# First attention of a hybrid block: another way for one transpose, mask and maximum in one operation, and TensorE's order as written

## The chip, the cores and the metric

The kernel runs on one core of one Trainium2 chip. A core has five engines that run side by side and wait for each other by semaphores: TensorE (PE; its weight loads are listed apart as PEld), VectorE (DVE), ScalarE (ACT), GpSimd (POOL) and SyncE (SP), which here only issues transfers between DRAM and the on-chip memory. TensorE writes to PSUM, eight banks of 512 fp32 numbers for each of 128 partitions; the other data is in SBUF. The metric is the device time of one execution in microseconds, the median of several.

## The reference

The program is one block on `x` of shape (4, 512, 512): `x += attention_a(layernorm(x))`, then a feed-forward with ternary weights, then a second attention with block-scaled weights, then the feed-forward again. The change is inside the first of the four. Cut to what it computes (16 query heads, 4 key heads that each serve a group of 4, width 128):

```python
q, k, v = x @ Wq, x @ Wk, x @ Wv                    # per head
qs, ks = softmax(q, -1), softmax(k, -1)             # over the head's width
gl = log_sigmoid(k) / 16
def step(S, inp):                                   # over the 512 positions
    q_t, k_t, v_t, g_t = inp
    S = S * exp(g_t)[..., None] + k_t[..., None] * v_t[..., None, :]
    return S, einsum('bhk,bhkv->bhv', q_t, S)
_, o_gla = scan(step, S0, (qs, ks, v, gl))
scores = rotary(q) @ rotary(k).T * 128 ** -0.5      # causal mask, softmax
y = softmax(where(causal, scores, min)) @ v
return (0.5 * y + 0.5 * o_gla).reshape(b, n, -1) @ Wo
```

## The kernel before

`first_attention_gentle` works on the sequence in chunks of 128 rows. The scan becomes matrix products: inside a chunk with queries and keys that carry the decay up to their row (`qd`, `kd`), across chunks with a `state` for each chunk. There are 16 groups, one for each of 4 sequences and 4 key heads, and 4 chunks in a group, so 64 chunks; chunk number `c` in its group sees `c + 1` blocks of keys.

A group (class `Group`) projects keys and values (`project`, four times), makes the gates (`gates`, L386 on), the decays (`decays`: two matmuls, `down`, `held`, rotated keys `kr`, decayed keys `kd`), transposes `kr` and `kd` (`transposes`) and makes the states (`states`). A chunk (class `Chunk`) goes through seven stages:

- `A`: projection of four query heads, `mm<-wq,xnT`, copied by ScalarE to `q_t`.
- `B`: softmax of the queries times decay, `qd` (L338 to L344), and rotated queries `qr` (L329 to L332, half of it on GpSimd).
- `C`: `qr` and `qd` are transposed by TensorE, four 128x128 transposes each (L350), and copied out of PSUM by ScalarE (L351) to `qrT` and `qdT`.
- `own`: scores of the decayed queries and keys inside the chunk (L458), masked by VectorE (L460).
- `D(h)`, for each of four heads: scores (L468), the causal mask added to the last 128 columns in PSUM (L469), the negated row maximum (L472), exponential with sum (L475), reciprocal, division (L477), a transpose of 32x32 blocks by VectorE into `turned` (L478). With the last head, one transfer writes `turned` to DRAM as `passed` (L481).
- `E`: four transfers read `passed` back as `prT`, so that the blocks land transposed (L487).
- `F`: GpSimd adds `own` to the last block (L493); TensorE multiplies queries by state (`pv<-qdT,state`, L496, not for `c = 0`) and adds `c + 1` products of values and weights (`pv<-prT,v_t`, L498); ScalarE halves and copies (L500).
- `G`: output projection, `mm<-wo,oT`, added to the residual by VectorE (L186).

A loop over `n` from -7 to 65 writes one step for each chunk: in step `n` chunk `n - 2` does `G`, `n - 1` does `F`, `n` does `E` and `own`, `n + 1` does `D`, `n + 2` does `C`, `n + 3` does `A` and `B`. `part` puts the group's work between, a quarter of it in a step, for a group that is used four to seven steps later. At the end of a step come pieces of work for later stages: a piece of `quantise` (a weight piece is read, and either its absolute values are summed or it is made ternary, L238 and L240, and stored to `blocks`, L242 and L244) and layernorms.

Each engine's instructions run in one fixed order. A planner makes this order when the program is built: it takes what it expects to be ready, the earlier written first, so that the order of TensorE, too, can differ from the written one. `in_place` (`keep_in_program_order`) keeps an instruction behind the one that was written just ahead of it on its engine; on SP it holds for `passed`, the reads of `E`, the reads of weight pieces and of `x`, not for the loads of `Wq`, `Wk`, `Wv`, `Wo`, the `ends` of decays and the stores of ternary blocks. Fp32 matmuls show as two instructions each in the profile. Score banks (`sc`) are three, `mm` two, `tp` two, `pv` one.

## Time and profile before

| what | value |
|---|---|
| time, median of 3 runs | 2508.99 us (2508.98 to 2510.9) |
| time of the profiled execution | 2506.09 us |
| its span, first to last instruction | 2504.3 us |
| mean granted TensorE clock | 0.997 |
| PE, DVE, ACT, POOL busy over the span | 98%, 66%, 49%, 16% |
| first attention, from the start to its last output projection | some 1080 us |
| PE, DVE, ACT busy in those 1080 us | 1042, 827, 662 us |
| moved by DMA | 333.5 MB, mean 133 GB/s |

In a group's row, `out<-in` names the tiles, then shapes and the count; after the bar come the busy time and the mean of one in ns, then the idle time of the engine before these instructions and what ended it. A row with `SPq` is a transfer that SP issues; its duration is the issue, not the transfer. The timeline gives the start, the duration and the instruction, like ones in a row merged. Matmuls overlap their neighbours, so their true cost is the distance between starts.

### The profile page before, as it was taken

To read this page: it belongs to the slowest core of one execution; us is meant where nothing else is said; L and a number is where in the kernel's file an instruction comes from. 1 tells how busy PE (TensorE), PEld (TensorE's weight loads), DVE (VectorE), ACT (ScalarE), POOL (GpSimd) and SP (SyncE) were. 2 spreads that over 40 slices of the span, in tenths; PEclk is the share of its full clock that TensorE was granted. 3 is DMA by queue.
4 is the path that set the end of the run, shared out by engine and by line. 5 is a ranking of instruction groups with operands and counts; after the bars stand their busy time and mean duration, and the time that the engine had idled before them with its cause. 6 is when DMAs were issued, how large, how long until landed. Compare 5 with 4: busy or idle time off the path is not lost.

```text
span 2504.3 us, 29057 instructions
## 1 busy us (share of the span) xinstructions
PE 2453.3 (98%) x8808; PEld 1569.9 (63%) x8808; DVE 1661.5 (66%) x3767; ACT 1234.2 (49%) x3114; POOL 392.0 (16%) x424
## 2 busy tenths in 40 slices
PE   7999999999999999999999999999999999999998
PEld 5555555555555555568886666666666666668887
DVE  5787778777887778645557666666766666654332
ACT  5766666666666666433325545444444444432222
POOL 1221212212222222112223333100000000000000
PEclk9999999999999999999999999999999999999999
DMA  3555555555555453565426777544443434333000
GB/s 114 152 174 143 169 143 158 165 156 143 146 152 150 145 151 118 160 205 155 131 81 187 185 205 213 153 121 107 112 122 93 130 88 131 89 93 130 18 18 19
DMA packets 194150, 333.53 MB, mean 133 GB/s; under 512 B 36032, under 2 KB 88640, under 8 KB 187840
## 3 DMA queue, kind: packets, MB, share of 16 engines
q1 hardware_dynamic: 185008, 305.01, 43.0%
q0 software_dynamic: 7680, 25.17, 3.5%
q8 instruction: 73, 1.20, 0.2%
q10 hardware_dynamic: 1296, 1.39, 0.2%
q14 instruction: 93, 0.76, 0.1%
HBM read 192.76 MB, written 71.57 MB: 106 GB/s over the span
## 4 chain that ended last, share of the span: by engine, by line
PE 79%; DVE 9%; issue 5%; ACT 3%; DMA 2%; POOL 1%; SPq 1%; POOLq 0%; ACTq 0%; DVEq 0%
PE mm L181 39%; PE sc L181 10%; PE sc L851 9%; PE tp L885 4%; PE pv L885 4%; PE pv L498 4%; PE sc L468 4%; PE tp L350 2%; PE sc L458 1%; PE pv L496 1%; DVE qd L344 1%; DVE nm L472 1%; PE tp L160 1%; DVE turned L478 1%; ACT pr L475 1%
## 5 line engine op out<-in xcount | busy, mean ns | idle before, releaser
L856 ACT ACTIVATE pr<-sc,nm 128x512 f32<-128x512 f32 x256 | 175.8, 687 | 303.1 <-DVE nm L853 259.7
L181 PE MATMUL sc<-xnhi,block 128*128 128x512 f32 x704 | 277.6, 394 | 2.8 <-ACT hT L1057 2.1
L181 PE MATMUL sc<-xnlo,block 128*128 128x512 f32 x704 | 274.6, 390 | 0.0
L851 PE MATMUL sc<-kT,qT 128*128 128x512 f32 x512 | 262.1, 594 | 0.0
L181 PE MATMUL mm<-xnhi,w 128*128 128x512 f32 x512 | 253.9, 496 | 0.0
L181 PE MATMUL mm<-wo,oT 128*128 128x512 f32 x512 | 231.4, 593 | 0.7 <-ACT oT L500 0.7
L181 PE MATMUL mm<-wq,xnT 128*128 128x512 f32 x512 | 231.8, 593 | 0.1
L853 DVE TENSOR_REDUCE nm<-sc 128x1 f32<-128x512 f32 x256 | 175.0, 683 | 74.4 <-PE sc L851 72.2
L475 ACT ACTIVATE pr<-sc,nm 128x128 f32<-128x128 f32 (+3 forms) x256 | 133.5, 522 | 153.6 <-DVE nm L472 138.7
L181 PE MATMUL mm<-xnlo,w 128*128 128x512 f32 x512 | 205.9, 402 | 0.0
L873 DVE STREAM_TRANSPOSE turned<-pr 128x512 f32<-128x512 f32 x256 | 173.3, 696 | 38.8 <-ACT pr L863 35.5
L331 POOL TENSOR_TENSOR sw<-q_t,turn 128x256 f32<-128x256 f32 x128 | 101.8, 816 | 524.2 <-ACT q_t L440 433.6
L468 PE MATMUL sc<-krT,qrT 128*128 128x512 f32 (+3 forms) x512 | 179.0, 435 | 2.6 <-ACT pr L475 2.6
L863 ACT ACTIVATE pr<-pr,den 128x512 f32<-128x512 f32 x192 | 138.4, 722 | 77.3 <-DVE den L861 77.0
L478 DVE STREAM_TRANSPOSE turned<-pr 128x128 f32<-128x128 f32 (+3 forms) x256 | 128.0, 505 | 66.0 <-ACT pr L477 62.8
L477 ACT ACTIVATE pr<-pr,den 128x128 f32<-128x128 f32 (+3 forms) x256 | 140.6, 558 | 55.8 <-DVE den L476 54.8
L181 PEld LDWEIGHTS mm<-wo,oT 128*128 128x128 f32 x512 | 96.2, 190 | 99.7 <-issue 95.6
L181 PEld LDWEIGHTS mm<-wq,xnT 128*128 128x128 f32 x512 | 95.3, 190 | 99.7 <-issue 93.7
L498 PE MATMUL pv<-prT,v_t 128*128 128x512 f32 x320 | 148.8, 594 | 7.4 <-POOL prT L493 7.4
L181 PEld LDWEIGHTS sc<-xnhi,block 128*128 128x128 f32 x704 | 132.2, 188 | 33.3 <-ACT hT L1057 3.9
L181 PEld LDWEIGHTS sc<-xnlo,block 128*128 128x128 f32 x704 | 132.3, 188 | 27.2 <-issue 0.5
L468 PEld LDWEIGHTS sc<-krT,qrT 128*128 128x128 f32 x512 | 92.0, 191 | 89.1 <-issue 72.9
(151 smaller groups left out, 4903.9 us busy)
## 6 DMA issues: line engine op xcount, KB each, us to landing
prT<-turned SPq DMA_DIRECT2D x1024, 64.0 KB, 2.0
w<-exact SPq DMA_DIRECT2D x32, 1024.0 KB, 5.4
wq<-in_Wq SPq DMA_DIRECT2D x16, 1024.0 KB, 7.2
wo<-in_Wo SPq DMA_DIRECT2D x16, 1024.0 KB, 5.3
passed<-turned SPq DMA_DIRECT2D x16, 1024.0 KB, 4.6
prT<-passed SPq DMA_DIRECT2D x64, 256.0 KB, 5.3
passed<-turned SPq DMA_DIRECT2D x16, 768.0 KB, 4.0
prT<-passed SPq DMA_DIRECT2D x64, 192.0 KB, 4.5
```

The lines of the kernel that those rows point to most:

```text
L181: nc.tensor.matmul(acc, lhsT=lhs(k), rhs=rhs(k), start=k == 0, stop=k == n - 1)
L468: nc.tensor.matmul(sc.rearrange("p q (k j) -> p q k j", j=32), lhsT=self.qrT[:, h, :], rhs=self.k.krT.rearrange("p (k q j) -> p q k j", q= ...
L475: nc.scalar.activation(pr, flat, AF.Exp, bias=nm, accum_out=den)
L477: nc.scalar.mul(pr, pr, den)
L478: nc.vector.transpose(self.turned.rearrange("p (q h x) -> p q h x", q=4, h=HG)[:, :, h, :], pr.rearrange("p (q x) -> p q x", q=4))
L498: nc.tensor.matmul(acc.rearrange("p h (a t) -> p h a t", a=4), lhsT=self.k.v_t[:, j, :], rhs=self.wts[:, :, :, j, :], start=j == c == 0, s ...
L851: nc.tensor.matmul(sc, lhsT=qTs[u][:, i * P : (i + 1) * P], rhs=kTs[u], start=True, stop=True)
L853: nc.vector.tensor_reduce(nm, sc, AX.X, ALU.max, negate=True)
L856: nc.scalar.activation(pr, sc, AF.Exp, bias=nm, accum_out=den)
L863: nc.scalar.mul(pr, pr, den)
L873: nc.vector.transpose(turns[u][:, :, i, :], pr.rearrange("p (q k) -> p q k", q=4))
L885: nc.tensor.matmul(accs[u].rearrange("p (n t) -> p n t", t=32), lhsT=v_ts[m, j][:, h * D : (h + 1) * D], rhs=prTs[u].rearrange("p a i (k t ...
```

## The change

Of each chunk, `qd` is no longer transposed by TensorE. `B` transposes its 32x32 blocks with one VectorE operation into a new tile `turned`, and a transfer writes it to DRAM as `queries`. A new stage `L`, written at the head of the next step for chunk `n + 2`, ahead of `E`, reads it back with four transfers as `qdT`; both are kept in written order on SP. `qdT` has its columns in blocks of 32, and the two matmuls that read it take a strided view. `C` keeps the transposes of `qr`.

The causal mask becomes a tile of 4 x 128 columns, zero but for the last 32 of each; `D` adds it to all columns of the scores, negates them and takes the row minimum in one VectorE operation, `tensor_tensor_reduce`, and the exponential gets the scale -1.

In `gates` the negated absolute value is made by ScalarE (`Abs`, with the scale -1 in the exponential) and no longer by VectorE.

The loop stands inside `manual_schedule` for TensorE: its instructions keep the order in which they are written. The load of `Wq` is written right behind the last `A` that uses the old one, and a group is made, and its `Wk` and `Wv` are loaded, at the third quarter of the group before.

```diff
-            causal = late.tile([P, P], F32, tag="causal", name="causal")
-            nc.scalar.dma_start(causal, a["causal"])
+            causal = two.tile([P, 4, P], F32, tag="causal", name="causal", bufs=1)
+            nc.vector.memset(causal, 0.0)
+            nc.scalar.dma_start(causal[:, :, 96:], a["causal"].rearrange("p (q j) -> p q j", q=4))
...
-                    nc.vector.scalar_tensor_tensor(gate, k_t, -1.0, k_t, ALU.mult, ALU.min)
-                    nc.scalar.activation(gate, gate, AF.Exp)
+                    nc.scalar.activation(gate, k_t, AF.Abs)
+                    nc.scalar.activation(gate, gate, AF.Exp, scale=-1.0)
...
-                    self.qd = two.tile([P, HG, D], F32, tag="qd", name="qd")
-                    softmax_decayed(self.qd, self.q_t, lambda h: self.k.down[:, c, :])
+                    qd = one.tile([P, HG, D], F32, tag="qd", name="qd")
+                    softmax_decayed(qd, self.q_t, lambda h: self.k.down[:, c, :])
+
+                    turned = one.tile([P, 4, HG, 32], F32, tag="turned", name="turned")
+                    nc.vector.transpose(turned.rearrange("p q h t -> p h q t"), qd.rearrange("p h (q j) -> p h q j", q=4))
+                    self.queries = dram.tile([P, HG * D], F32, tag="queries", name="queries", bufs=3)
+                    in_place(nc.sync.dma_start(self.queries, turned.rearrange("p q h t -> p (q h t)")))
...
+                def L(self):
+                    qdT = two.tile([P, 4, HG, 32], F32, tag="qdT", name="qdT", bufs=4)
+                    for q in range(4):
+                        in_place(nc.sync.dma_start(qdT[32 * q : 32 * (q + 1)].rearrange("j a h t -> j a (h t)"), self.queries.rearrange("(a j) (q x) -> q j a x", a=4, q=4)[q]))
+                    self.qdT = qdT.rearrange("p a h t -> p h a t")
...
-                    self.qdT = two.tile([P, HG, P], F32, tag="qdT", name="qdT", bufs=4)
-                    transposed(self.qdT, self.qd, nc.scalar.copy)
...
-                    nc.tensor.matmul(sc, lhsT=self.k.kdT[:, self.c, :], rhs=self.qdT, start=True, stop=True)
+                    nc.tensor.matmul(sc.rearrange("p h (a t) -> p h a t", a=4), lhsT=self.k.kdT[:, self.c, :], rhs=self.qdT, start=True, stop=True)
...
-                    nc.vector.tensor_tensor(sc[:, :, 32 * c :], sc[:, :, 32 * c :], causal.rearrange("p (q j) -> p q j", q=4), ALU.add)
...
-                    nc.vector.tensor_reduce(nm, flat, AX.X, ALU.max, negate=True)
+
+                    nc.vector.tensor_tensor_reduce(sc, sc, causal[:, :, 32 * (3 - c) :], -1.0, 3e38, ALU.add, ALU.min, nm)
...
-                    nc.scalar.activation(pr, flat, AF.Exp, bias=nm, accum_out=den)
+                    nc.scalar.activation(pr, flat, AF.Exp, bias=nm, scale=-1.0, accum_out=den)
...
-                    if p == half == 0:
-                        groups[m] = Group(*divmod(m, KV))
...
+            groups[0] = Group(0, 0)
+            with tc.manual_schedule(engines={mybir.EngineType.PE}):
+                for n in range(-7, last + 2):
...
+                    if y:
+                        y.L()
+                    if w:
+                        w.E()
+                    part(m, p, 0)
...
+                    if y:
+                        y.C()
+                    if x:
+                        x.D(0)
+                    if z and n > -2:
+                        z.A()
+
+                    if n in range(0, last - NC, NC):
+                        groups[n // NC + 1].load_wq()
+                    if x:
+                        x.D(1)
+                    if v:
+                        v.F()
+                    if p == 3:
+                        next(ln, None)
+                    if z:
+                        z.B()
+                    if x:
+                        x.D(2)
+                    if w:
+                        w.own()
+                    if p == 2 and m + 1 < B * KV:
+                        groups[m + 1] = Group(*divmod(m + 1, KV))
...
-                if n in range(0, last - NC, NC):
-                    groups[n // NC + 1].load_wq()
```

The lines of the loop that are not shown keep their content and their order; they stand one level deeper.

More of the change, by code (lines that the diff above doesn't have):

```diff
@@ L363, in __init__ @@
                     self.b, self.g = b, g
-                    self.xnT = xnTs[b]
                     self.wkv = one.tile([P, NK, 2 * D], F32, tag="wkv", name="wkv")
@@ L380, in project @@
                     acc = bank("mm", [P, 2, D])
-                    project(acc.rearrange("p a d -> p (a d)"), lambda k: self.xnT[:, k, c * P : (c + 1) * P], lambda k: self.wkv[:, k, :])
+                    project(acc.rearrange("p a d -> p (a d)"), lambda k: xnTs[self.b][:, k, c * P : (c + 1) * P], lambda k: self.wkv[:, k, :])
                     nc.scalar.copy(self.k_t[:, c, :], acc[:, 0, :])
@@ L437, in A @@
                     acc = bank("mm", [P, HG, D])
-                    project(acc.rearrange("p h d -> p (h d)"), lambda k: self.k.xnT[:, k, self.c * P : (self.c + 1) * P], lambda k: self.k.wq[:, k, :])
+                    project(acc.rearrange("p h d -> p (h d)"), lambda k: xnTs[self.k.b][:, k, self.c * P : (self.c + 1) * P], lambda k: self.k.wq[:, k, :])
                     self.q_t = two.tile([P, HG, D], F32, tag="q_t", name="q_t")
@@ L495, in F @@
                     if c:
-                        nc.tensor.matmul(acc, lhsT=self.k.state[:, c - 1, :], rhs=self.qdT, start=True, stop=False)
+                        nc.tensor.matmul(acc.rearrange("p h (a t) -> p h a t", a=4), lhsT=self.k.state[:, c - 1, :], rhs=self.qdT, start=True, stop=False)
                     for j in range(c + 1):
@@ L530, in first_attention_gentle @@
             ln = iter(())
-            for n in range(-7, last + 2):
-                m, p = divmod(n + 7, NC)
-                at = lambda i: chunks.get(n + i) if n + i < last else None
-                if (m + 1) % KV == 0 and (m + 1) // KV < B:
-                    if p == 0:
-                        load((m + 1) // KV)
-                    if p == 2:
-                        ln = normalise((m + 1) // KV)
-                    if p > 1:
-                        next(ln)
-                u, v, w, x, y, z = (at(i) for i in range(-2, 4))
-                if p == 0:
-                    part(m - 1, 4, 0)
-                if w:
-                    w.E()
-                part(m, p, 0)
-                if n == -6:
-                    nc.scalar.dma_start(turn, a["turn"])
-                    fill_until()
-                if y:
-                    y.C()
-                if x:
-                    x.D(0)
-                if z and n > -2:
-                    z.A()
-                if x:
-                    x.D(1)
-                if v:
-                    v.F()
-                if p == 3:
-                    next(ln, None)
-                if z:
-                    z.B()
-                if x:
-                    x.D(2)
-                if w:
-                    w.own()
-                if n in (-6, -5):
-                    if n == -6:
-                        groups[0].load_wq()
-                        chunks.update((c, Chunk(groups[0], c)) for c in range(2))
-                    chunks[n + 6].A()
-                part(m, p, 1)
-                if u:
-                    u.G()
-                if x:
-                    x.D(3)
-                if n in range(0, last - NC, NC):
-                    groups[n // NC + 1].load_wq()
-                if n in (-2, *range(NC + 1, last, NC)):
-                    groups[max(n // NC, 0)].load_wo()
-                if p > 1:
-                    next(ln, None)
-                if n > -4:
-                    next(quant, None)
-                for f in extra.get(n, ()):
-                    f()
@@ new lines, in first_attention_gentle @@
+            groups[0] = Group(0, 0)
+            with tc.manual_schedule(engines={mybir.EngineType.PE}):
+                for n in range(-7, last + 2):
+                    m, p = divmod(n + 7, NC)
+                    at = lambda i: chunks.get(n + i) if n + i < last else None
+                    if (m + 1) % KV == 0 and (m + 1) // KV < B:
+                        if p == 0:
+                            load((m + 1) // KV)
+                        if p == 2:
+                            ln = normalise((m + 1) // KV)
+                        if p > 1:
+                            next(ln)
+                    u, v, w, x, y, z = (at(i) for i in range(-2, 4))
+                    if p == 0:
+                        part(m - 1, 4, 0)
+                    if y:
[3 more added lines that the diff above has]
+                    part(m, p, 0)
+                    if n == -6:
+                        nc.scalar.dma_start(turn, a["turn"])
+                        fill_until()
+                    if y:
[20 more added lines that the diff above has]
+                        groups[m + 1] = Group(*divmod(m + 1, KV))
+                    if n in (-6, -5):
+                        if n == -6:
+                            groups[0].load_wq()
+                            chunks.update((c, Chunk(groups[0], c)) for c in range(2))
+                        chunks[n + 6].A()
+                    part(m, p, 1)
+                    if u:
+                        u.G()
+                    if x:
+                        x.D(3)
+                    if n in (-2, *range(NC + 1, last, NC)):
+                        groups[max(n // NC, 0)].load_wo()
+                    if p > 1:
+                        next(ln, None)
+                    if n > -4:
+                        next(quant, None)
+                    for f in extra.get(n, ()):
+                        f()
```

## The prediction

> **What bounds the kernel now.** I read the page first: engine shares, then the 40 slices.

> ```profile
> span 2504.3 us, 29057 instructions
> PE 2453.3 (98%) x8808; PEld 1569.9 (63%) x8808; DVE 1661.5 (66%) x3767; ACT 1234.2 (49%) x3114; POOL 392.0 (16%) x424
> PE   7999999999999999999999999999999999999998
> PEclk9999999999999999999999999999999999999999
> ```

> TensorE is busy 98% of the span and the clock is granted nearly everywhere, so the time is TensorE's work plus its waits. The change touches only the first attention, which ends at 1080 us (its last `mm<-wo,oT` matmuls start at 1075.5 us in the timeline). So the next view is the busy times by stretch:

> ```profile
> 60.00:1078.00 1018.00, 996.73 (x3320) 554.43 (x3319) 791.76 (x2046) 629.04 (x1894) 210.40 (x218) 1.00 0.51 149
> ```

> The columns are length, then busy time of PE, PEld, DVE, ACT, POOL, granted clock, DMA share, GB/s. Inside the attention PE lacks 1018.0 - 996.7 = 21.3 us; DVE is at 78%, ACT at 62%. What a PE instruction costs is the distance of starts in the timeline, because the busy sums overlap: four `tp<-ident,qd` transposes take 0.43 us (157.72 to 158.16), a four-matmul projection 3.44 us (158.38 to 161.82). Everything that can be won here is transposes, 64 x 0.437 = 28.0 us, and waits, 21.3 us.

> **The parts that take work away.** The rows by shape:

> ```profile
> L478 DVE STREAM_TRANSPOSE turned<-pr 128x512 f32<-128x512 f32 x64 | 45.3, 707 | 21.5 <-ACT pr L477 21.2
> L472 DVE TENSOR_REDUCE nm<-sc 128x1 f32<-128x512 f32 x64 | 43.5, 680 | 0.6
> L460 DVE TENSOR_TENSOR own<-sc,until 128x512 f32<-128x512 f32 x64 | 42.9, 671 | 0.2
> L350 PE MATMUL tp<-ident,qd 128*128 128x128 f32 x256 | 39.4, 274 | 0.7 <-ACT qrT L351 0.4 <-DVE qd L344 0.3
> L351 ACT COPY qdT<-tp 128x512 f32<-128x512 f32 x64 | 37.8, 591 | 1.1 <-PE tp L350 1.1
> ```

> PE loses the `qd` transposes: -28.0 us on the path. ACT loses 64 x 0.591 = 37.8 us and gains 16 x 0.63 for `Abs` (row of L390: 627 ns) = 10 us. DVE loses the 16 gate operations of 988 ns (15.8 us) and gains 64 transposes like L478, 64 x 0.707 = 45.2 us. The mask (289 ns, x256 = 73.5 us) and the four widths of the maximum (280, 414, 549, 680 ns, x64 each = 123 us) become one custom operation that the trace doesn't have. From below it costs the maximum alone, from above twice the maximum (123 to 246 us); the nearest row is L460, a two-source operation out of PSUM, 671 ns at 512, so I take that width's price at each width plus 82 ns for reading the accumulator (row of L293): 64 x (0.29 + 0.42 + 0.55 + 0.67 + 4 x 0.082) = 145 us. DVE then sums to 827 - 196 + 145 + 45 - 16 = 805 us of some 1065: still under PE, so 0 us on the path. What covers it is the 22% of DVE that is free. With the upper bound DVE has 906 us, 85%, and the cover gets thin.

> [...] The rows say what the rest is: a 256 KB write (`passed` of that size lands after 3.3 us), four 64 KB reads (3.5 us), five issues on SP. The result is wanted two steps after it is begun, some 31 us, so its landing costs 0 us; without that cover, 7 us for each chunk. [...]

> **What is queued on SP.** SP issues in order; four `prT` reads took it 2.00 us. The change puts `L`, four reads, ahead of `E`, the reads of the transposed probabilities, and one write ahead of `passed`: 5 x 0.48 = 2.4 us of a 15.7 us step. In most steps `E` is still waiting for `passed` to land then, and `L` is hidden. Not so in the 27 steps in which the weights are made ternary: there the store of a ternary block was written just ahead of `L` and `E`, and they are pinned behind it. One such step, on SP, PE and POOL:

> ```profile
> 162.87 0.34 SPq L481 DMA_DIRECT2D passed<-turned  x1
> 163.31 0.38 SPq L216 DMA_DIRECT2D w<-in_w1T  x1
> 171.25 0.48 SPq L407 DMA_DIRECT2D ends<-down  x1
> 171.82 0.54 SPq L242 DMA_DIRECT2D blocks<-tern  x1
> 172.47 2.00 SPq L487 DMA_DIRECT2D prT<-passed  x4
> ```

> ```profile
> 156.43 1.02 PE L468 MATMUL sc<-krT,qrT 128*128 128x512 f32 x2
> ...
> 178.31 1.02 PE L496 MATMUL pv<-qdT,state 128*128 128x512 f32 x2
> ...
> 186.81 3.60 PE L498 MATMUL pv<-prT,v_t 128*128 128x512 f32 x8
> ```

> ```profile
> 180.73 1.27 POOL L493 TENSOR_TENSOR prT<-prT,own 128x512 f32<-128x512 f32 x1 [0.53 <-PE sc L468]
> ```

> This is chunk 7, the last of its sequence. Its last score matmul `D(3)` starts at 156.43; `passed` has landed at 167.5, but the reads go out at 172.47, behind the store at 171.82, which waits for the weight load at 163.31 and VectorE. The data is there at 180.6. The planner had moved `F` far back, to 186.81, so nothing waits.

> **TensorE in written order.** Now `F` of this chunk stands where it is written. From the end of `D(3)`: one step of 13.3 us (transposes 0.44, four narrow scores 0.86, projection 3.43, `F` of chunk 6 3.43, `own` 0.86, decays 0.86, output projection 3.43), then 0.44 + 0.43 + 3.43 + 0.43 = 4.7, then the state matmul 0.86: the probabilities are wanted after 18.9 us, at 157.3 + 18.9 = 176.2. They come at 180.6: 4.4 us late. The same reading of chunks 11, 23, 27, 43, 47 and 51, the other last chunks in ternary steps, gives 1.8 to 6.6 us, mean 4.5. With `L`'s 1.9 us issued in front it is 6.4. VectorE may get to the ternary operation earlier when PE waits, so I take 5.0: 7 x 5.0 = +35 us. Behind the waiting matmul stand `D(2)`, `own`, the output projection and `D(3)`, and with `D(3)` the next `passed`: the wait moves everything, and is not made good. Outside these steps the last chunks' data landed 16.5 to 19.8 us after `D(3)` started, against 19.7: no wait, or barely.

> Here the clock speaks against the change:

> ```profile
> 54.00:60.00 6.00, 2.84 (x13) 1.80 (x14) 5.67 (x19) 5.22 (x21) 1.42 (x2) 0.98 0.58 174
> 60.00:64.00 4.00, 4.00 (x16) 2.92 (x15) 3.90 (x16) 3.44 (x14) 0.00 (x0) 0.60 0.34 91
> 64.00:68.00 4.00, 4.00 (x21) 2.95 (x20) 2.34 (x12) 2.35 (x7) 0.00 (x0) 1.00 0.71 224
> ```

> After a stretch with waits (the longest 2.6 us) the granted clock is 0.60 over 4 us: 1.6 us lost. [...]

> The other edits of the order: the layernorm transposes now follow their VectorE operation at once (one such wait is in the trace, 1.36 us): 12 of them, 0 to 2 us each, +8. A projection behind the residual addition, `F` of first chunks: +5. At the end of the attention the planner had put 22 feed-forward matmuls into the gap before the last `F`; in order, `F` of chunk 63 stands 7.7 us of work behind its `D(3)` and needs data that took 18 us: 0 to +8, I take 6. The start: all four layernorm transposes before the first projection, 0 to 8, I take 2. `Wq` loads at once after the last use (landing left 4.5 to 10.3 us before the next use), `Wk`/`Wv` load half a step group earlier and find their buffer free: 0. `Abs` on ACT and the mask's zero fill: 0.

> Sum: -28.0 - 21.3 (all old waits are counted anew) + 35 + 6 + 8 + 5 + 6 + 2 = +12.7 us. The profiled execution took 2506.1 us, 1.8 around the span, and lies 2.9 below the median; the difference goes onto the median: 2509.0 + 12.7 = 2522 us.

> **Rivals.** (a) The waits don't come: VectorE makes the ternary block right behind its load (3 us were between landing and end in the step shown, 8 in others), `E` goes out when `passed` lands, and `F` in its written place is fed. Then 35 + 6 fall away: -28 us, 2481, and 2470 if layernorm and the tail cost nothing either. For it: only 27 of 64 steps are held up, and the old order had waits of its own because the planner judged landings wrongly. Against it: the store stays pinned ahead. It decides where the wait of a last chunk is under 1 us. (b) VectorE becomes the bound: the custom operation costs twice the maximum, DVE goes to 85%, scores are freed late, and PE in fixed order can't do anything else meanwhile: some 0.6 us a step, +40 on top, 2562. For it: the price is unknown; against it: L460 and L472 cost the same. (c) Gain and waits cancel, within 0.2% (5 us, about what a measurement of this kernel can tell from no change).

> **How the numbers follow.** The forecast 0.52, its own range 2514 to 2545; (a) 0.36, 2468 to 2503; (b) 0.08; (c) 0.04. Faster 0.36, same 0.04, slower 0.52 + 0.08 = 0.60. The range reaches from the middle of (a) to (b): 2474 to 2565.

> **What would show it.** Right: PE has no `tp<-ident,qd`; in the ternary stretches (145 to 265, 405 to 530, 720 to 895 us) PE waits of 3 us and more on `pv<-prT` for DMA or POOL, and single dips of the clock; SP issues `qdT` between `blocks` and `prT`. DVE near 805 us up to the end of the attention. Wrong: `pv` waits under 10 us in all, an end of the attention before 1055 us; or VectorE above 85% with PE waiting for `sc`.

## The result, and the profile after

The changed kernel takes 2545.3 us (2541.5 to 2552.5), the kernel before 2509.2 us on the same chip: a ratio of 1.0146, 95% interval 1.0119 to 1.0172. It is slower by 36 us. The forecast was 2522, slower, with a range from 2474 to 2565. One execution of experiment 1 below took 2581.9 us at a lower granted clock (0.94) and is left out. The profiled executions are 2548.6 and 2506.1 us, 42.5 us apart, and nearly all of that has arisen when the last `mm<-wo,oT` of the attention starts: at 1118.9 us now, at 1078.6 before.

The page of the changed kernel, engine shares, and then its busy times over the attention (the columns as in the prediction's view):

```profile
span 2546.7 us, 28941 instructions
PE 2456.7 (96%) x8552; PEld 1553.5 (61%) x8552; DVE 1663.7 (65%) x3816; ACT 1213.9 (48%) x3066; POOL 388.5 (15%) x424
...
60.00:1118.00 1058.00, 999.39 (x3085) 537.91 (x3084) 796.31 (x2100) 612.66 (x1861) 208.59 (x220) 0.97 0.60 175
```

256 PE instructions are gone, and yet the attention is 40 us longer: PE lacks 58.6 us in this stretch where it lacked 21.3, and the granted clock is 0.97 where it was 1.00. The waits of TensorE, up to 1120 us (what was waited for, total us, times, longest):

```profile
PE pv L508 <- POOL prT L503: 39.7, 19, 3.9
PE tp L160 <- DVE xn L157: 19.3, 8, 9.0
PE pv L508 <- DMA prT<-passed: 2.8, 4, 1.1
```

Before, the same `pv` wait was 7.4 us in 5 times, the `tp` wait 15.9 in 7. The new time stands behind GpSimd's addition into the transposed probabilities, the first operation of `F`.

To compare kernels I split the time from the first TensorE instruction to the last `mm<-wo,oT` by distances between starts: what an instruction takes when nothing holds it (0.43 us for each of the two instructions of an fp32 matmul of 128x512, 0.11 for a transpose) is work; of what is above that, up to half of the time in stretches with a halved clock is clock; the rest is waits. It is worked out from the traces, one profiled execution each, and small terms are good to a few us.

| | median us | last `wo,oT` starts | work | clock | waits | of these `pv` | `tp<-ident,xn` |
|---|---|---|---|---|---|---|---|
| before | 2509.2 | 1078.6 | 1020.5 | 3.1 | 46.3 | 9.0 | 10.2 |
| after | 2545.3 | 1118.9 | 993.1 | 26.8 | 90.1 | 52.7 | 15.0 |
| difference | +36.1 | +40.3 | -27.4 | +23.7 | +43.8 | +43.7 | +4.8 |

The 27.4 us of transposes came out. The waits took 44 and the clock 24.

What one such wait looks like, chunk 6 (the third of its sequence), on SP, then on GpSimd, then on TensorE:

```profile
148.66 0.40 SPq L378 DMA_DIRECT2D wo<-in_Wo  x1
154.87 0.33 SPq L491 DMA_DIRECT2D passed<-turned  x1
155.29 0.38 SPq L216 DMA_DIRECT2D w<-in_w1T  x1
164.44 0.37 SPq L242 DMA_DIRECT2D blocks<-tern  x1
164.90 2.25 SPq L458 DMA_DIRECT2D qdT<-queries  x4
167.26 1.79 SPq L497 DMA_DIRECT2D prT<-passed  x4
```

```profile
173.07 1.41 POOL L333 TENSOR_TENSOR sw<-q_t,turn 128x256 f32<-128x256 f32 x2 [12.59 <-ACT q_t L441]
176.49 1.45 POOL L333 TENSOR_TENSOR sw<-k_t,turn 128x256 f32<-128x256 f32 x2 [2.01 <-DVE den L344]
177.90 1.30 POOL L503 TENSOR_TENSOR prT<-prT,own 128x512 f32<-128x512 f32 x1
```

```profile
174.06 1.96 PE L508 MATMUL pv<-prT,v_t 128*128 128x512 f32 x4 [0.92 <-DMA prT<-passed]
179.26 1.13 PE L508 MATMUL pv<-prT,v_t 128*128 128x512 f32 x2 [3.24 <-POOL prT L503]
```

`passed` had landed at 158.8. The reads stand behind the query reads, those behind the ternary store, and the store behind a weight load issued at 155.29, which lands at 159.8, and VectorE's ternary operation, which ends at 164.4. So the reads go out 8.4 us after their data was in DRAM; I call this time the hold. The data is on the chip at 173.9. By then GpSimd has begun the rotation of chunk 10's queries, and the planner put the key rotation of the next group, which waits for VectorE, ahead of the addition. TensorE waits 3.24 us for it, after 0.92 for the data. The halved clock that comes with such a wait (chunk 42, TensorE idle for 3.5 us up to 782.1):

```profile
776.00:780.00 4.00, 2.60 (x7) 0.81 (x5) 3.82 (x10) 2.85 (x12) 2.57 (x3) 1.00 0.90 262
780.00:784.00 4.00, 1.91 (x3) 0.88 (x4) 4.00 (x7) 0.00 (x0) 2.04 (x3) 0.64 0.64 201
784.00:788.00 4.00, 4.00 (x9) 2.26 (x8) 2.51 (x7) 1.86 (x7) 0.00 (x0) 0.50 0.38 119
788.00:792.00 4.00, 4.00 (x17) 2.27 (x16) 1.98 (x7) 2.52 (x10) 0.00 (x0) 1.00 0.81 193
```

PE is "busy" 4.00 us at 784 with 9 matmuls and at 788 with 17: the busy share does not show what the clock takes. VectorE's new operations by shape:

```profile
L449 DVE STREAM_TRANSPOSE turned<-qd 128x512 f32<-128x512 f32 x64 | 45.1, 705 | 0.6
L482 DVE CUSTOM_DVE_ANT_0 sc<-sc,causal 128x512 f32<-128x512 f32 x64 | 44.2, 691 | 7.2 <-PE sc L478 7.1
L482 DVE DVE_READ_ACCUMULATOR2_ANT nm<- 128x1 f32 x256 | 35.5, 139 | 0.0
```

With the narrower widths (557, 422 and 295 ns) mask and minimum cost 125.8 + 35.5 = 161 us.

### The profile page after: what moved, and what is told of

The parts are those of the page before. It is cut to its first block, busy times and chain, and to the rows that moved or that the text cites. A ratio compares the mean times of both kernels' runs of the same rounds, so it can differ in the third digit from the quotient of the medians.

```text
span 2546.7 us, 28941 instructions
## 1 busy us (share of the span) xinstructions
PE 2456.7 (96%) x8552; PEld 1553.5 (61%) x8552; DVE 1663.7 (65%) x3816; ACT 1213.9 (48%) x3066; POOL 388.5 (15%) x424
## 4 chain that ended last, share of the span: by engine, by line
PE 71%; DVE 10%; issue 9%; ACT 3%; DMA 3%; POOL 3%; SPq 2%; POOLq 0%; ACTq 0%; DVEq 0%
PE mm L181 36%; PE sc L181 10%; PE sc L865 8%; PE tp L899 4%; PE pv L899 4%; PE sc L478 3%; PE pv L508 2%; DVE qd L346 1%; PE sc L468 1%; SPq L892 1%; PE tp L352 1%; POOL sw L333 1%; POOL prT L503 1%; PE tp L160 1%; DVE sc L482 1%
## 5 line engine op out<-in xcount | busy, mean ns | idle before, releaser
L508 PE MATMUL pv<-prT,v_t 128*128 128x512 f32 x320 | 162.4, 625 | 43.5 <-POOL prT L503 39.7
L478 PE MATMUL sc<-krT,qrT 128*128 128x512 f32 (+3 forms) x512 | 182.8, 441 | 0.3 <-ACT pr L485 0.3
L487 ACT ACTIVATE pr<-pr,den 128x128 f32<-128x128 f32 (+3 forms) x256 | 140.7, 558 | 44.1 <-DVE den L486 43.4
L478 PEld LDWEIGHTS sc<-krT,qrT 128*128 128x128 f32 x512 | 94.2, 195 | 92.5 <-issue 81.5
L181 PEld LDWEIGHTS sc<-xnlo,block 128*128 128x128 f32 x704 | 132.8, 189 | 27.5 <-issue 0.5
```

The lines of the kernel that those rows point to most:

```text
L181: nc.tensor.matmul(acc, lhsT=lhs(k), rhs=rhs(k), start=k == 0, stop=k == n - 1)
L478: nc.tensor.matmul(sc.rearrange("p q (k j) -> p q k j", j=32), lhsT=self.qrT[:, h, :], rhs=self.k.krT.rearrange("p (k q j) -> p q k j", q= ...
L487: nc.scalar.mul(pr, pr, den)
L508: nc.tensor.matmul(acc.rearrange("p h (a t) -> p h a t", a=4), lhsT=self.k.v_t[:, j, :], rhs=self.wts[:, :, :, j, :], start=j == c == 0, s ...
```

## The experiments

All times are medians, and each ratio is to the kernel before on the same chip, with its 95% interval.

**1. The application later.** `F` behind the output projection:

```diff
-                    if v:
-                        v.F()
...
                     if u:
                         u.G()
+                    if v:
+                        v.F()
```

> F is written behind the output projection and ahead of D(3), everything else as in the changed kernel. Theory (waits): the changed kernel loses 44 us more on pv<-prT than the old one and 24 us more on the halved clock that follows such waits; F comes some 6 us later now, so pv waits fall from 53 us to under 12, the halved clock from 27 us lost to under 8, and the time from 2545 to about 2485 (2475 to 2500), faster than before. Rival (the transfers and VectorE's extra transposes hold everything back, whatever the place of F): the wait moves to another matmul, time above 2530.

2533.0 us, 1.0103 (1.0083 to 1.0123): 11 us gained where about 60 were expected. `pv` waits fell from 52.7 to 22.2 us, clock only to 23.8. What remained changed its cause:

```profile
PE tp L160 <- DVE xn L157: 27.8, 10, 9.0
PE pv L508 <- DMA prT<-passed: 19.9, 6, 4.2
```

Six waits for the data itself, at chunk 10 and the last chunks 11, 27, 43, 47 and 51: there the reads were still held on SP for 8 to 14 us after `passed` had landed, and TensorE started within 0.2 us of their landing. Moving the consumer covers GpSimd, not SP.

**2. The ternary store later**, written one step behind the operation that makes its block, the application where the change has it:

```diff
+                yield
                 if n < 2:
                     nc.sync.dma_start(blocks[f : f + m, :, n, ...
...
-                yield
```

> The store of a ternary block is written one step later, ahead of the next weight load, so that L and E are no longer pinned behind a store that waits for VectorE. Theory (store): E goes out within 1 us of passed's landing in all steps (now 5 to 11 us in the ternary ones), pv waits fall from 53 us to about 15, time about 2500. Rival (GpSimd): the data comes earlier but the addition stays behind the rotation of the keys on GpSimd; pv waits stay above 30 us, time above 2525.

2514.7 us, 1.0024 (1.0014 to 1.0034): 31 us gained, most of the loss. The reads of chunk 6 are now issued 0.1 us after `passed` lands, where they were 8.4 us late. `pv` waits 27.2, clock 16.6. No other single edit gains as much time. Of the `pv` waits that stay, 17.7 us end with GpSimd's addition.

**3. GpSimd in written order too.**

```diff
-            with tc.manual_schedule(engines={mybir.EngineType.PE}):
+            with tc.manual_schedule(engines={mybir.EngineType.PE, mybir.EngineType.Pool}):
```

> GpSimd too keeps its written order, so that the addition to prT stands ahead of the rotation of the next group's keys. Theory (store): the addition can't start before the data, which stays 8 us late; of a wait of 4.2 us for a third chunk 1 to 2 us stay, those of first and last chunks stay; pv waits 25 to 35 us, time 2515 to 2530. Rival (GpSimd): its order is the cause; pv waits under 15 us, time about 2500.

2537.5 us, 1.0119 (1.0100 to 1.0138). `pv` waits fell to 24.1, but the layernorm waits rose from 15.0 to 25.9, and scores and projections waited 11 us. So GpSimd's order holds the addition up: fixing it takes away as much of the `pv` waits as experiment 2, but most of that gain goes to other waits.

**4. TensorE in the planner's order**, all else as changed:

```diff
-            with tc.manual_schedule(engines={mybir.EngineType.PE}):
+            with ExitStack():
```

> The changed kernel without the fixed order of TensorE: the planner orders it as before. Theory (waits in fixed order): the planner moves F back as in the old kernel; the 28 us of the transposes stay won, pv waits near the old 9 us, time 2480 to 2495. Rival (the way through DRAM costs it): 2510 or more with waits on qdT, prT or sc.

2587.7 us, 1.0329 (1.0308 to 1.0349): over 40 us slower than with the written order, where 50 to 65 faster was expected. Clock loss falls to 16.1, waits rise to 141.5:

```profile
PE pv L506 <- ACT oT L510: 27.4, 17, 3.2
PE sc L478 <- ACT pr L485: 21.0, 31, 1.7
PE pv L508 <- POOL prT L503: 14.7, 13, 2.6
```

TensorE waits for `pv`'s one bank and for the score banks to come free. So with the other edits in place the planner's order fits worse than the written one, and the idea that the written order alone did the harm was wrong. Why the planner chose this order was not followed up.

**5. The written order alone**, on the kernel before (its loop put into the same `manual_schedule`, nothing else changed):

> The kernel before, with nothing changed but TensorE's instructions of the first attention fixed in written order. Theory 1, the written order itself makes the waits: 2555 us, that is the time of the changed kernel plus the 27 us of transposes, less some 2 us at each of seven waits since no query reads stand on SP; pv waits of 30 us or more. Theory 2, the query reads on SP make the waits: 2510 to 2520 us, pv waits near the 9 us of before.

2543.5 us, 1.0136 (1.0119 to 1.0153). The order costs the old kernel 36 us. In the profiled execution, which at 2550.2 us lies 7 above the median, waits go from 46.3 to 69.9 and clock from 3.1 to 18.8. `pv` waits are 21.3, less than the 30 named, and they are the ones that the prediction had described. Chunk 11, the last of its sequence, on SP and then on PE:

```profile
240.92 0.34 SPq L481 DMA_DIRECT2D passed<-turned  x1
241.31 0.43 SPq L216 DMA_DIRECT2D w<-in_w1T  x1
249.00 0.47 SPq L407 DMA_DIRECT2D ends<-down  x1
249.57 0.54 SPq L242 DMA_DIRECT2D blocks<-tern  x1
250.21 2.01 SPq L487 DMA_DIRECT2D prT<-passed  x4
```

```profile
254.34 1.02 PE L496 MATMUL pv<-qdT,state 128*128 128x512 f32 x2
258.42 5.37 PE L498 MATMUL pv<-prT,v_t 128*128 128x512 f32 x8 [3.05 <-DMA prT<-passed]
```

With experiment 4 this gives all four corners: neither 2509; order alone +36; the other edits alone +81; both +36. The two are not additive.

**6. TensorE's transposes back** in the changed kernel (no `turned` of the queries, no `queries`, no `L`):

```diff
-                    nc.vector.transpose(turned.rearrange("p q h t -> p h q t"), ...
-                    in_place(nc.sync.dma_start(self.queries, ...
...
+                    transposed(qdT, self.qd, nc.scalar.copy)
...
-                    if y:
-                        y.L()
```

> Changed kernel, with the decayed queries transposed by TensorE again (no VectorE transposes, no write, no reads); order, mask and everything else as changed. Theory 1, the route by way of DRAM is hidden and worth its 27 us of TensorE work, but its four reads on SP lengthen the waits by about 2 us in each ternary step where the reads are late: 2545 + 27 - 14 = 2558 us. Theory 2, the query reads on SP are what holds the probabilities: waits fall to the level before, 2545 + 27 - 60 = 2512 us.

2540.9 us, 1.0134 (1.0117 to 1.0150): without its main part the change takes the same time, within the intervals, as with it (1.0119 to 1.0172). Work is back at 1020.6, but `pv` waits are 17.3 instead of 52.7 and clock 16.7 instead of 26.8. So in this order the route by way of DRAM costs 35 us of `pv` waits and 10 of clock, and takes away 27.5 us of work and 11 of other waits (7.7 of them at the `qd` transposes themselves): together it gains nothing. How it makes the `pv` waits is on SP, where chunk 6 is handled now like this:

```profile
143.26 0.40 SPq L378 DMA_DIRECT2D wo<-in_Wo  x1
143.75 0.45 SPq L216 DMA_DIRECT2D w<-in_w1T  x1
148.70 0.33 SPq L484 DMA_DIRECT2D passed<-turned  x1
152.06 0.38 SPq L242 DMA_DIRECT2D blocks<-tern  x1
152.58 2.19 SPq L490 DMA_DIRECT2D prT<-passed  x4
```

The weight load is issued ahead of `passed`, so the ternary block is made and stored by 152.4 and the reads go out when `passed` has landed. In the changed kernel the load came behind `passed`, and the store with all that follows it had to wait for that load and for VectorE. It is so in every third chunk of a ternary step (6, 10, 22, 26, 42, 46 and 50): with the written order alone (5) and here the load is ahead of `passed` in all seven, and the hold is at most 1.1 us; in the changed kernel it is behind in all seven, and the hold is 8.0 to 9.5 us. Third chunks are special because only in their steps the load of `Wo` is written between `passed` and the weight load, so that the weight load is pinned to `Wo` and can go ahead of `passed`. The waits moved from last chunks, where they are here and in 5, to third chunks for that reason. What in the route makes the planner place the load later was not isolated.

**7. Each weight block loaded one step earlier** in the changed kernel:

```diff
                 nc.vector.scalar_tensor_tensor(t, w, up, low, ALU.is_gt, ALU.subtract)
+                if i + 1 < len(pieces[n]):
+                    w = piece(n, *pieces[n][i + 1])
```

> Changed kernel, with each weight block loaded one step before it is made ternary, so that the load stands a whole step ahead on SP; the application and the store stay where the changed kernel has them. Theory 1, the changed kernel's long waits come from the late load: it was issued behind the passed write, so the store behind it, the query reads and the probability reads all stood 8 us too long on SP: the hold falls under 3 us, pv waits from 53 to under 15 us, half-clock loss by 10 us: 2500 us. Theory 2, VectorE comes to the ternary operation late by its own order: the hold stays at 5 us or more, 2535 us or above.

2523.7 us, 1.0071 (1.0054 to 1.0087), between the two theories. Where it could act, the hold fell from 6 to 9.5 us to about 1 (chunk 10 from 9.5 to 1.3, 26 from 8.4 to 0.3, for 50 it is 0.5, for 42 still 2.5), and the 3 to 3.7 us waits of chunks 10, 26, 46 and 50 shrank to under 1 us. The first two blocks of a weight are loaded in the same step, so for chunks 6 and 22 the hold stayed at 8.3 us; their waits grew, to 4.7 and 5.0 us. GpSimd's order added its part there as before (rows of POOL, then of PE, chunk 6):

```profile
178.37 1.45 POOL L335 TENSOR_TENSOR sw<-k_t,turn 128x256 f32<-128x256 f32 x2 [2.43 <-DVE qr L336]
179.78 1.30 POOL L505 TENSOR_TENSOR prT<-prT,own 128x512 f32<-128x512 f32 x1
```

```profile
181.14 2.07 PE L510 MATMUL pv<-prT,v_t 128*128 128x512 f32 x2 [4.69 <-POOL prT L505]
```

`pv` waits are 38.8 in all, not under 15. By the ratios the late load, as far as this edit cures it, is half of the loss. The other half stays, with `pv` waits at the first blocks, behind GpSimd's order and at the start of the attention.

**8. Both late edits** (1 and 2 together):

> Changed kernel, with the application of the probabilities written after the output projection and the ternary store written one step later (the two edits tried singly before, 2533.9 and 2514.7 us). Theory 1, the reads of the transposed probabilities are held on SP behind the ternary store and the written order wants them too early: the two cures meet the same 44 us of waits from both ends, so they overlap, but together they remove nearly all of it: pv waits under 8 us, half-clock loss under 12 us, layernorm waits of about 20 us stay: 2495 us. Theory 2, what was left (17 to 22 us of pv waits) has another cause, such as the order on GpSimd or VectorE: no better than the store alone, 2515 us.

2505.4 us, 0.9989 (0.9982 to 0.9996): all of the loss is gone. `pv` waits are 1.3 us: together the two edits cover whatever makes them. But clock stayed at 18.1, and waits for VectorE grew: layernorm 17.9, key and value projections 7.9, `qr` transposes 5.5. 10 us of the expected gain went there.

**9. And the layernorm rows ahead.** In the attention VectorE's `xn` of a chunk is written one call before TensorE's transposes of it, and the calls of the last two steps of a group are moved apart to fit:

```diff
+        if ahead:
+            yield
+            xn = scaled(0)
...
             sink(c, tp)
+            if ahead and c < NC - 1:
+                xn = scaled(c + 1)
```

> As the run with both late edits, and the layernorm's normalised rows of each sequence written on VectorE one call ahead of TensorE's transposes of them. Theory 1, each of three sequences waits 2.6 to 4.5 us for VectorE there and pays another 1.7 us to the halved clock: about 13 us less than the run with both edits alone, 2482 us. Theory 2, VectorE is the queue that is late: the wait only moves to scores or to the gates, same time as the run with both edits.

2494.2 us, 0.9947 (0.9930 to 0.9964). This beats both kernels, 13 us under the old one; the last edit gave 11 of the 13 us expected. In the attention clock is 11.1 and waits 49.5.

**10. The route's worth once the waits are gone**: version 9 with TensorE's transposes back, as in 6.

> The fastest version so far (both late edits and the layernorm rows ahead, 2494.2 us), with the decayed queries transposed by TensorE again instead of by VectorE and DRAM. Theory 1, with the waits gone the route is worth its whole TensorE work: 2494 + 27 = 2521 us. Theory 2, the route brings waits of its own wherever it stands: 2500 to 2510 us. (Taking the route out of the changed kernel itself made that 4 us faster.)

2506.0 us, 0.9995 (0.9985 to 1.0005). The route is worth 12 us here, not 27: work is 27.6 us less with it, but waits are 10.4 and clock 3.7 us more. Those waits are many and small, nearly all for VectorE, which does 38 us more in the whole program with the route (1641.7 against 1603.7). That this is their cause was not isolated further.

**11. Mask and minimum as two operations** in version 9 (and the exponential without its scale of -1):

```diff
-                    nc.vector.tensor_tensor_reduce(sc, sc, causal[:, :, 32 * (3 - c) :], -1.0, 3e38, ALU.add, ALU.min, nm)
+                    nc.vector.tensor_tensor(sc[:, :, 32 * c :], sc[:, :, 32 * c :], causal[:, :, 96:], ALU.add)
+                    nc.vector.tensor_reduce(nm, flat, AX.X, ALU.max, negate=True)
```

> The fastest version so far (2494.2 us), with mask and row minimum as the two VectorE operations of the kernel before. By the rows of the two kernels VectorE gets 36 us more work (197 us against 126 + 35). Theory 1, TensorE covers VectorE: within 4 us of 2494. Theory 2, scores come free late and the fixed order hands that on: 0.3 to 0.6 us in each of 64 steps, 2513 to 2532 us.

2503.1 us, 0.9983 (0.9973 to 0.9992). VectorE has 35.6 us more work, as reckoned, and the kernel takes 9 us more (by the intervals some 4 to 14): waits +7.7, clock +1.7. Neither theory held: VectorE, busy 774 us of the 1000 from 60 to 1060 us in version 9 and 808 here, is not the bound, and yet about a quarter of its work came through. TensorE waits for a score bank that comes free late:

```profile
PE tp L167 <- DVE xn L152: 15.7, 6, 9.0
PE sc L487 <- ACT pr L495: 5.8, 6, 2.2
```

In version 9 the second of these was 1.7 us. That the fixed order, in which TensorE can't do something else meanwhile, is what hands it on was not tried separately.

**12. The threshold's sum later** in version 9 (a `yield` between VectorE's row sum and TensorE's sum over the partitions):

> The fastest version so far (2494.2 us), with the TensorE sum over the partitions of a weight's threshold written one step behind VectorE's row sum. Theory 1, the three waits of that matmul (3.1 us together) and the one behind it for VectorE's threshold (2.5 us twice, with the halved clock after it) go: 2487 us. Theory 2, the steps of the ternary blocks move against the groups and new waits take their place: 2494 us or more.

2491.3 us, 0.9940 (0.9923 to 0.9956): inside the interval of version 9. The 3.1 us of waits at that matmul are gone, `sc<-qdT,kdT` waits rose from 3.9 to 9.3, and clock fell by 2.8. It is no slower, and whether it is faster is not settled.

## Why the prediction was right, and where it was wrong

The direction came, and the signs that it named: seven steps with some 3 us or more of waits on `pv<-prT` in the ternary stretches, halved clocks behind them, and `qdT` issued between `blocks` and `prT`. The size did not: the sum was +12.7 us, and the traces show +40.3 at the end of the attention. The 2545.3 us lie at the upper end of the forecast's own range (2514 to 2545); the wide range, 2474 to 2565, would have held no change too. By its own steps:

- **Transposes, -28.0.** Right: -27.4. Starts in the timeline were the right price, and the landing of the queries is hidden: TensorE never waits for `qdT`.
- **Waits, -21.3 + 35 + 8 + 5 + 6 + 2 = +34.7.** Measured +43.8: the size is near in part by luck, since the places are not those of the forecast. The waits at `F` in ternary steps behind the store pinned on SP came, seven of them, 26.4 us together (forecast 35). They stand at third chunks, not at last ones. The step that failed is the reading of the old trace's SP order as if it would stay: the prediction looked at last chunks only, counted what `L` adds to SP in issue time (1.9 us) and left the weight load where it was. In the steps of third chunks the load went behind `passed` all seven times (in the kernel before, only at 10, 26, 46 and 50), and its landing and VectorE's work came in front of the reads (experiments 6 and 7). The last chunks then waited only 0 to 1.3 us, since TensorE had already been set back. The last-chunk mechanism itself was sound: in the old kernel with the order alone (5) it is there at chunks 11, 27, 43, 47 and 51, with 1.8 to 4.3 us.
- The prediction had `F` wait for a DMA or GpSimd, and put only the data's landing in its sum. GpSimd's place in line is its own term: key rotations ahead of the addition, some 4 us between landing and its start at chunk 6. And it had nothing for the start of the attention, 6.4 us in three `pv` waits before 112 us. Outside the ternary steps it expected no wait, or barely one; nine chunks (3, 14, 15, 19, 30, 31, 38, 55 and 58) waited there for GpSimd's addition, 0.8 to 1.9 us each, 11 us together.
- The term -21.3 took all old waits away. Of those that are neither `pv` nor layernorm, 27.1 us by the table, 22.4 are still there.
- **The clock, +6.** Measured +23.7, the largest mis-sized term. No run shows the +6, which was the author's estimate. The row-based 1.6 us per wait, 11 us for seven, was for one stretch; seven of the twelve stretches before 1118 us last 6.8 us, at up to 3.4 us each, and waits of 2.3 us had them follow as well. Five of the twelve came with TensorE idle for 3.48 to 3.92 us, the other seven with gaps of 1.96 to 3.24 us. The row was right in sign and too small.
- **Layernorm +8**: +4.8. **Tail +6**: 0.5 us, the last application waited only that long, and the same 24 feed-forward matmuls as before stand ahead of it. Both terms are over-estimates that hid part of the others' shortfall.
- **VectorE, 805 us in the attention, 0 on the path.** Measured 829 up to 1118 us, with 139 ns for the accumulator's reading where 82 was taken; 691 ns against 671 at the full width. It was not the bound, but the zero was too good: in experiment 11 about a quarter of a VectorE saving reached the end, and the small waits for VectorE in 10 suggest the same for what the transposes add.
- **Rivals.** (a) did not come. Edits that put the store, the application and the layernorm rows elsewhere came near it: 2494, where it had 2481. (b) did not come: mask and minimum cost 161 us against 145 forecast and 246 at worst.

## What to carry to other kernels

Before an engine is put into written order, follow every queue that feeds it, and ask of each in-order queue what stands ahead of the transfer that matters; a new transfer can change the order of its neighbours and not just their issue times (here the weight load came to stand behind `passed` in all seven third chunks of ternary steps, and the reads were held for 8.0 to 9.5 us). The cure was to write the ternary store later, the consumer later and VectorE's input ahead. The store alone won back 31 of the 36 us; only with the other two did the kernel come out clearly under the old time, since each cure showed the next wait. Price a wait on TensorE with the halved clock behind it: here the clock took 23.7 of the 40.3 us.

## What the runs showed of the hardware that was not expected

```profile
779.41 3.04 DVE L346 SCALAR_TENSOR_TENSOR qd<-qd,den,down 128x128 f32<-128x128 f32 x4
```

  Over the fourteen traces, 2951 of these operations had GpSimd idle all the time, and none took over 0.36 us. 601 had it busy for over half of the time, and 448 of them took over 0.6 us, up to 1.44. Why GpSimd's work goes with the slower operations was not tried.
- **The accumulator's reading costs 139 ns** here behind the custom operation and 82 ns in another row of the kernel before: with 256 of them, 15 us of VectorE.
